# Four residual layers on one core: one more set of a recurrence's idle-time gate products, a full last block and ten fuller blocks ahead of it

## The chip, the cores and the metric

The kernel runs on one core of a Trainium2 chip. The metric is device microseconds of one execution; the profile is one execution taken by the hardware profiler. Where the text says PE it means TensorE, PEld its weight loads, DVE is VectorE, ACT ScalarE, POOL GpSimd, SP the queue that issues most DMAs.

## The reference

`x` is (16 batches, 512 steps, 512 features), `cond` is (16, 512), all float32. Four layers are added to x in turn:

```python
x = x + L0(x)    # wavelet analysis and synthesis with one gate per batch and feature: x + (x + x * gate)
x = x + L1(x)    # h = tanh(x_t @ Wx + b + h_prev @ Wh), 512 steps in sequence
x = x + L2(x)    # gates of all steps:
    f = sigmoid(x @ W_f.T + b_f); i = sigmoid(x @ W_i.T + b_i)
    s = f + i + EPS; f, i = f / s, i / s
    new = i * (x @ W_h.T + b_h)
    # log-cumulative sums of f and a scaled cumulative sum of new over the steps
x = x + L3(x)    # x + x @ (base + A_b @ B_b.T), a layer of rank 8 made per batch
```

L2's gates need only the finished x of the same step, so they can be computed while L1 is still working on later steps. That is what the change is about.

## The kernel before

**Two stages.** The first, lines 567 to 673, runs L0 and the recurrence L1: 64 blocks (`NBLK`) of 8 steps (`T`), all 16 batches at once. The second, the loop over batches behind `rnn.close()`, runs L2 and L3 batch by batch. Features stand in four chunks (`KC`) of 128 partitions. The result of the first stage, `x2`, stays on the chip as [128, 4, 16, 512].

**A step of the recurrence.** PE adds sixteen products of the previous h with `wh_sb` (L417, each of 32 columns, four beside each other) into a PSUM bank that already holds the input products; ACT takes tanh in four pieces (L609), DVE transposes each (L610), and the next step's products can begin. Behind its own products a step issues filler: input products of the next block (`inputs`, by the table `SHARE`; from block 17 on, four of sixteen in each odd step and none in the even ones), and parts of gates (`early_gate`).

**Parts and sets.** A set in `SETS` is (four batches, 128 steps, one chunk of 128 features) in all but the first few. It takes twelve parts: for f, i and the candidate four each, one for each chunk of the contraction. A part is four products of 512 columns (L465; float32, so each is two instructions on PE), with 32 output partitions each, side by side. `PARTS` says which steps of a block take a part; the sets are worked off in the order of the list. From block 17 to 62 that is steps 0, 2, 4, 6, in the last block 0, 2, 3, 4, 6. Input products end with block 62, since there is no next block.

**What follows a part.** After the fourth part of f its sigmoid runs on ACT six steps later, after the fourth of i at once (both L479), through `timed`. DVE then has sixteen pieces for a set: two sums (L489), eight reciprocals of 64 columns (L492), two products with f and two with i (L496), and, as `urgent`, two candidate products (L500). `do_pieces` takes one piece in each step, two in the last two blocks, and what is left is done behind the loop, ahead of `add_base` (L539), which makes batch 0's layer. Finished f and i go to `early` in DRAM from SP (L483). The PSUM of f, i and candidate alternates between two banks.

**The second stage.** `gate_unit(b, j)` computes one chunk of one batch. `made_before` gives the number of steps `te` that the sets have covered; for those f and i are loaded from `early` (SP, L715), and PE computes only columns `te` to 512 (L700: 24 instructions a unit, of 512 - te columns). ACT takes the sigmoids (L716), DVE sums, inverts, multiplies (L717 to L722) and runs three scans over all 512 columns (L726, L730, L732), POOL adds (L736, L737) into `x3`. Batches 0 to 7 have te = 128, 128, 144, 160 in their four chunks, batches 8 to 15 have 192, 192, 144, 160. After the second unit of a batch, PE runs the last product of the batch before (`last_layer`, L756), whose four tiles ACT copies (L751, two buffers `osb`) and SP stores (L752). Engines work their instructions off in order, so ACT's sigmoids of the third unit stand behind the copies, and a store on SP stands behind the loads of f and i that were issued before it; those wait for a free buffer (three for f, two for i).

Of the kernel before, what the change touches and what calls it, by code (L numbers as in the profile page):

```python
# [37 lines left out]
KC = D // P  # L38
R = 8

T = 8
NBLK = S // T
# [14 lines left out]
FIRST, SECOND, MAIN = 16 // T, 32 // T, 128 // T + 1  # L57
SETS = [(slice(0, 16), slice(0, 16), KC - 2), (slice(0, 16), slice(0, 32), KC - 1)]
# [2 lines left out]
SETS += [(slice(b, b + 4), slice(0, 128), j) for b in (0, 4) for j in range(KC - 2)]  # L61
SETS += [(slice(b, b + 4), slice(16, 144), KC - 2) for b in (0, 4, 8, 12)]
SETS += [(slice(b, b + 4), slice(32, 160), KC - 1) for b in (0, 4, 8, 12)]
SETS += [(slice(b, b + 4), slice(64, 192), j) for b in (8, 12) for j in (0, 1)]

PARTS = [()] * FIRST + [(0, 1, 3, 4, 5, 7)] * (SECOND - FIRST) + [(0, 2, 4)] * (MAIN - SECOND) + [(0, 2, 4, 6)] * (NBLK - MAIN - 1) + [(0, 2, 3, 4, 6)]
TE = 192


def made_before(b, j):  # L70
# [13 lines left out]
def kernel(  # L84
# [27 lines left out]
    def col(which, j):  # L112
        return vec_sb[:, which * KC + j : which * KC + j + 1]
# [16 lines left out]
    dram = ctx.enter_context(tc.tile_pool(name="dram", bufs=1, space=bass.MemoryType.DRAM))  # L130
    early = dram.tile([B, 2, KC, P, TE], F32, name="early")
    bias_a = dram.tile([R, D], F32, name="bias_a")
# [236 lines left out]
    def layer_part(i, k):  # L369

        if k == 0:
            layer_part.ps = ps_p.tile([P, P], F32, tag="pf", name=f"pf_{i}")
            if i:
                which, r = LAYERS[i]
                layer_part.bias = w2pool.tile([P, P], F32, tag="b2", name=f"b2_{i}", bufs=2)
                row = (bias_a, b2b)[which][r].rearrange("(j o p) -> j o p", j=KC, o=1)
                nc.sync.dma_start(out=layer_part.bias, in_=row.to_broadcast([KC, BP, P]))
        columns, src = (straight, hT3) if i else (tile_columns, aeT)
        for j in range(KC):
            nc.tensor.matmul(  # L380
                layer_part.ps[j * BP : (j + 1) * BP, :],
                src[:, k, :],
                columns(chunk_sb[i * KC + k], j),
                start=(k == 0),
                stop=(k == KC - 1),
                skip_group_check=True,
            )
        load_chunk()
# [46 lines left out]
    timed, urgent, pieces = {}, [], []  # L435
# [9 lines left out]
    def early_gate(q, step):  # L445

        u, k = divmod(q, KC)
        number, which = divmod(u, 3)
        batches, steps, j = SETS[number]
        shape = dict(b=batches.stop - batches.start, t=steps.stop - steps.start)  # L450
        width = shape["b"] * shape["t"]
        first = number < NSETS
        if k == 0:

            pool, tag = ((ps_q, "pg"), (ps_p, "pf"))[0 if first else (u - 3 * NSETS) % 2]
            early_gate.ps = pool.tile([P, WIDE], F32, tag=tag, name=f"pg_{u}")[:, :width]
            if which == 0:
                early_gate.tiles = [
                    w2pool.tile([P, WIDE], F32, tag=name, name=f"{name}_{number}")[:, :width]
                    for name in ("ef", "ei", "es")  # L460
                ]
        ps = early_gate.ps
        w = (wf_sb, wi_sb, wc_sb)[which]
        for c in range(KC):
            nc.tensor.matmul(  # L465
                ps[c * BP : (c + 1) * BP, :].rearrange("p (b t) -> p b t", **shape),
                w[:, k, j * P + c * BP : j * P + (c + 1) * BP],
                x2[:, k, batches, steps],
                start=(k == 0),
                stop=(k == KC - 1),  # L470
                skip_group_check=True,
            )
        if k < KC - 1:
            return
        f, i, s = early_gate.tiles
        halves = [slice(at, at + WIDE // 2) for at in range(0, width, WIDE // 2)]

        def sigmoid(gate, bias):
            nc.scalar.activation(gate, ps, AF.Sigmoid, bias=col(bias, j))  # L479

        def store(which, got, at):
            n = slice(at.start // shape["t"], at.stop // shape["t"])
            nc.sync.dma_start(  # L483
                out=early[batches, which, j, :, steps].rearrange("b p t -> p b t")[:, n],
                in_=got.rearrange("p (b t) -> p b t", **shape)[:, n],
            )

        def total(at):
            nc.vector.scalar_tensor_tensor(s[:, at], f[:, at], EPS, i[:, at], ALU.add, ALU.add)  # L489

        def invert(at):
            nc.vector.reciprocal(s[:, at], s[:, at])  # L492

        def normalize(which, at):
            got = (f, i)[which]
            nc.vector.tensor_tensor(got[:, at], got[:, at], s[:, at], ALU.mult)  # L496
            store(which, got, at)

        def times_candidate(at):
            nc.vector.scalar_tensor_tensor(  # L500
                i[:, at], ps[:, at], col(C_BH, j), i[:, at], ALU.add, ALU.mult
            )
            if at is halves[-1]:
                pieces.extend(lambda at=at: normalize(1, at) for at in halves)

        def end_input_gate():
            sigmoid(i, C_BI)
            early_gate.sums = [lambda at=at: total(at) for at in halves]
            pieces.extend(early_gate.sums)
            for n in range(0, width, WIDE // 8):  # L510
                pieces.append(lambda at=slice(n, n + WIDE // 8): invert(at))
            pieces.extend(lambda at=at: normalize(0, at) for at in halves)

        if which == 0:

            timed.setdefault(step if first else step + 6, []).append(lambda: sigmoid(f, C_BF))
        elif which == 1:
            timed.setdefault(step, []).append(end_input_gate)
        else:

            assert not any(job in pieces for job in early_gate.sums)
            urgent.extend(lambda at=at: times_candidate(at) for at in halves)
# [42 lines left out]
    for n in range(NBLK):  # L565
# [3 lines left out]
        for s in range(T):  # L569
# [16 lines left out]
            if s in LAYER_STEPS[n]:  # L586
                layer_part(n, LAYER_STEPS[n].index(s))
            if s in PARTS[n]:
                early_gate(made, n * T + s)
                made += 1  # L590
# [27 lines left out]
            if s == max(PAIRS[g]):  # L618
                t0, t1 = PAIRS[g]
                step = t1 - t0  # L620
# [250 lines left out]
```

## Time and profile before

| | us |
|---|---|
| three runs | 1618.48, 1618.99, 1623.41 (median 1618.99) |
| the profiled execution | 1615.84 |
| its span, first to last instruction | 1614.1 |
| PE, PEld, DVE, ACT, POOL busy | 1603.6, 1146.0, 1132.3, 424.9, 172.6 |
| recurrence | to 909 us of the span |
| loop over batches | from 909 us on |
| granted TensorE clock | 1.000 |

The profile's page gives the busy time of each engine, the chain that ended last and the costliest groups. A group's line holds the source line, engine, operation, tiles and shape, then busy time, mean duration and idle time of the engine ahead of it with what ended it. The timeline lists instructions by start and length; runs of the same instruction are merged, and a number in brackets is idle time before it and its releaser.

### The profile page before, as it was taken

How to read it: one execution, taken by the hardware profiler on the slowest of the kernel's cores; microseconds unless marked ns; L12 is line 12 of the kernel's file. 1: busy time of each engine (PE TensorE's matmuls, PEld its weight loads, DVE VectorE, ACT ScalarE, POOL GpSimd, SP SyncE). 2: the span in 40 equal slices, each digit the busy share in tenths (PEclk: the TensorE clock that was granted, in tenths of full speed). 3: DMA queues.
4: the chain of work that ended last, by engine and by line, in shares of the span. 5: the costliest groups of instructions: out<-in, count | busy, mean ns of one | idle time of the engine just before them, and what ended most of it. 6: DMA issues, size and time to landing. Idle time of an engine off the chain costs nothing.

```text
span 1614.1 us, 67901 instructions
## 1 busy us (share of the span) xinstructions
PE 1603.6 (99%) x29328; PEld 1146.0 (71%) x29328; DVE 1132.3 (70%) x3618; ACT 424.9 (26%) x2484; POOL 172.6 (11%) x145
## 2 busy tenths in 40 slices
PE   9999999999999999999999999999999999999998
PEld 6888888888888888888888655555555555555564
DVE  4555655565556666666665798888888888988887
ACT  3333333333333333333333211111111111111111
POOL 0000000000000000000000022222222222222222
PEclk9999999999999999999999999999999999999999
DMA  7554431111111111111111101111111111111111
GB/s 228 148 147 128 121 105 46 36 31 36 37 37 37 37 37 37 37 37 31 37 39 30 29 21 43 33 43 39 43 40 44 44 46 39 31 44 47 37 44 58
DMA packets 128085, 88.11 MB, mean 55 GB/s; under 512 B 22645, under 2 KB 116633, under 8 KB 127785
## 3 DMA queue, kind: packets, MB, share of 16 engines
q1 hardware_dynamic: 79152, 55.05, 11.1%
q10 hardware_dynamic: 48632, 28.73, 6.2%
q8 instruction: 229, 3.75, 1.0%
q14 instruction: 72, 0.58, 0.1%
HBM read 55.67 MB, written 28.07 MB: 52 GB/s over the span
## 4 chain that ended last, share of the span: by engine, by line
PE 96%; DVE 2%; DMA 1%; issue 0%; SPq 0%; ACT 0%; ACTq 0%; DVEq 0%
PE pre L417 41%; PE po L756 13%; PE pg L465 13%; PE pf L700 9%; PE pc L700 9%; PE pi L700 9%; PE pf L380 1%; PE pl_layer L535 1%; DVE s L718 1%; DMA wh_sb<-in_wh_dram 1%; PE pl_last L756 0%; DMA xb<-in_xT_dram 0%; DVE s L726 0%; DVE s L730 0%; PE po_last L756 0%
## 5 line engine op out<-in xcount | busy, mean ns | idle before, releaser
L417 PEld LDWEIGHTS pre<-wh_sb,h_out 128*32 128x32 f32 x16384 | 466.7, 110 | 146.6 <-DVE h_out L610 143.4
L417 PE MATMUL pre<-wh_sb,h_out 128*32 128x128 f32 x16384 | 560.6, 273 | 2.4 <-DVE h_out L610 1.1
L610 DVE STREAM_TRANSPOSE h_out<-a 128x32 f32<-128x32 f32 x2048 | 264.6, 187 | 347.4 <-ACT a L609 345.9
L609 ACT ACTIVATE a<-pre 128x32 f32<-128x32 f32 x2048 | 238.0, 203 | 573.4 <-PE pre L417 572.7
L417 PE MATMUL pre<-wx_sb,x 128*32 128x128 f32 x8192 | 285.9, 273 | 1.0 <-DMA wx_sb<-in_wx_dram 0.5
L417 PEld LDWEIGHTS pre<-wx_sb,x 128*32 128x32 f32 x8192 | 239.0, 110 | 2.1 <-DMA wx_sb<-in_wx_dram 1.5
L756 PE MATMUL po<-wx_sb,x 128*128 128x512 f32 x480 | 209.0, 592 | 0.1
L756 PEld LDWEIGHTS po<-wx_sb,x 128*128 128x128 f32 x480 | 91.0, 190 | 111.6 <-issue 105.7
L700 PE MATMUL pf<-x,wf_sb 128*128 128x352 f32 (+3 forms) x512 | 165.3, 466 | 0.3 <-DVE x L622 0.3
L700 PE MATMUL pc<-x,wc_sb 128*128 128x352 f32 (+3 forms) x512 | 163.7, 463 | 1.3 <-DVE i L722 1.3
L700 PE MATMUL pi<-x,wi_sb 128*128 128x352 f32 (+3 forms) x512 | 163.6, 462 | 0.0
L718 DVE RECIPROCAL s<-s 128x368 f32<-128x368 f32 (+2 forms) x64 | 152.2, 2378 | 2.2
L700 PEld LDWEIGHTS pf<-x,wf_sb 128*128 128x128 f32 x512 | 96.0, 190 | 68.4 <-issue 15.8
L736 POOL TENSOR_TENSOR s<-s,f 128x512 f32<-128x512 f32 x63 | 86.5, 1374 | 509.9 <-DVE s L730 504.1
L700 PEld LDWEIGHTS pc<-x,wc_sb 128*128 128x128 f32 x512 | 97.2, 190 | 57.5 <-DVE i L722 1.9
L700 PEld LDWEIGHTS pi<-x,wi_sb 128*128 128x128 f32 x512 | 97.3, 190 | 55.9
L622 DVE TENSOR_TENSOR x<-x,h_out 128x128 f32<-128x128 f32 x256 | 101.2, 395 | 18.9 <-DMA wi_sb<-in_wiT_dram 0.2
L751 ACT COPY osb<-po 128x512 f32<-128x512 f32 x60 | 35.1, 585 | 263.4 <-PE po L756 144.9
L683 POOL MEMSET zero<- 128x1 f32 x1 | 0.1, 98 | 907.5 <-DVE wx_sb L539 907.5
L717 DVE SCALAR_TENSOR_TENSOR s<-f,i 128x368 f32<-128x368 f32 (+2 forms) x64 | 34.7, 543 | 88.1 <-ACT i L716 88.1
L716 ACT ACTIVATE f<-pf,vec_sb 128x368 f32<-128x368 f32 (+2 forms) x64 | 35.7, 558 | 215.2 <-PE pf L700 160.6
L465 PE MATMUL pg<-x,wc_sb 128*32 128x512 f32 (+1 forms) x640 | 84.2, 581 | 0.0
(113 smaller groups left out, 1270.8 us busy)
## 6 DMA issues: line engine op xcount, KB each, us to landing
out_dram<-osb SPq DMA_DIRECT2D x63, 256.0 KB
xb<-in_xT_dram ACTq DMA_DIRECT2D x61, 256.0 KB
w<-in_l3w_dram SPq DMA_DIRECT2D x72, 128.0 KB
w<-in_l3w_dram ACTq DMA_DIRECT2D x64, 128.0 KB
early<-ef SPq DMA_DIRECT2D x39, 128.0 KB
early<-ei SPq DMA_DIRECT2D x39, 128.0 KB
f<-early SPq DMA_DIRECT2D x16, 96.0 KB
i<-early SPq DMA_DIRECT2D x16, 96.0 KB
```

Of the source, the lines that this page charges most:

```text
L417: nc.tensor.matmul(pre[PLACE[g][0]][j * BP : (j + 1) * BP, PLACE[g][1], :], lhsT, tile_columns(w, j), start=False, stop=False, skip_group_ ...
L465: nc.tensor.matmul(ps[c * BP : (c + 1) * BP, :].rearrange("p (b t) -> p b t", **shape), w[:, k, j * P + c * BP : j * P + (c + 1) * BP], x2 ...
L609: nc.scalar.activation(a[:, at], pre[bank][:, place, at], AF.Tanh)
L610: nc.vector.transpose(turned[:, c, :], a[:, at])
L622: nc.vector.tensor_tensor(x2[:, :, :, at].rearrange("p k b t -> p k t b"), xs[n][:, :, t0 // 2, :, :], turned.rearrange("p k (t b) -> p k ...
L700: nc.tensor.matmul(p[:, te:], w_sb[:, k, j * P : (j + 1) * P], x2[:, k, b, te:], start=(k == 0), stop=(k == KC - 1),)
L716: nc.scalar.activation(gate[:, new], p[:, new], AF.Sigmoid, bias=col(bias, j))
L717: nc.vector.scalar_tensor_tensor(s[:, new], f[:, new], EPS, i[:, new], ALU.add, ALU.add)
L718: nc.vector.reciprocal(s[:, new], s[:, new])
L736: engine.tensor_tensor(s, s, f, ALU.add)
L751: nc.scalar.copy(osb, po)
L756: nc.tensor.matmul(po, x3[:, k, t * P : (t + 1) * P], layer[:, k, :], start=(k == 0), stop=(k == KC - 1))
```

## The change

One set is added in the list: steps 128 to 255 of batches 4 to 7 in chunk 0, ahead of the last four sets. `made_before` follows the list, so these four units get te = 256 in place of 128. The twelve parts that it needs are placed by `PARTS`: the last block takes a part in each of steps 0 to 6, and each of the ten blocks ahead of it takes one more in step 7, behind that step's input products. The buffer `early` in DRAM grows to 256 steps a row (`TE`). The sigmoid of f now runs at the latest in the step before the first part that writes the same PSUM bank again (`FIRST_PARTS`).

```diff
 SETS += [(slice(b, b + 4), slice(32, 160), KC - 1) for b in (0, 4, 8, 12)]
+SETS += [(slice(4, 8), slice(128, 256), 0)]
 SETS += [(slice(b, b + 4), slice(64, 192), j) for b in (8, 12) for j in (0, 1)]
 
-PARTS = [()] * FIRST + [(0, 1, 3, 4, 5, 7)] * (SECOND - FIRST) + [(0, 2, 4)] * (MAIN - SECOND) + [(0, 2, 4, 6)] * (NBLK - MAIN - 1) + [(0, 2, 3, 4, 6)]
-TE = 192
+PARTS = [()] * FIRST + [(0, 1, 3, 4, 5, 7)] * (SECOND - FIRST) + [(0, 2, 4)] * (MAIN - SECOND)
+PARTS += [(0, 2, 4, 6)] * (NBLK - MAIN - 11) + [(0, 2, 4, 6, 7)] * 10 + [tuple(range(T - 1))]
+TE = 256
+
+SLOTS = [n * T + s for n in range(NBLK) for s in PARTS[n]]
+FIRST_PARTS = SLOTS[::KC]
+assert len(SLOTS) == 3 * KC * len(SETS)
...
-            timed.setdefault(step if first else step + 6, []).append(lambda: sigmoid(f, C_BF))
+            late = step if first else min(step + 6, FIRST_PARTS[u + 2] - 1)
+            timed.setdefault(late, []).append(lambda: sigmoid(f, C_BF))
```

The sets behind the new one start twelve parts later in the count of parts, but the added places make up for that: the last set now has its parts in blocks 62 and 63, where it had them in blocks 61 to 63.

## The prediction

> **What bounds the kernel now.** I read the page first, then the groups by shape, then the timeline of PE by step and of all engines at two places.
>
> ```profile
> span 1614.1 us, 67901 instructions
> ...
> PE 1603.6 (99%) x29328; PEld 1146.0 (71%) x29328; DVE 1132.3 (70%) x3618; ACT 424.9 (26%) x2484; POOL 172.6 (11%) x145
> ...
> PE pre L417 41%; PE po L756 13%; PE pg L465 13%; PE pf L700 9%; PE pc L700 9%; PE pi L700 9%; PE pf L380 1%; PE pl_layer L535 1%; DVE s L718 1%; DMA wh_sb<-in_wh_dram 1%; PE pl_last L756 0%; DMA xb<-in_xT_dram 0%; DVE s L726 0%; DVE s L730 0%; PE po_last L756 0%
> ```
>
> The chain that ended last is 96% PE, in the recurrence (L417, L465, to 909 us) and behind it (L700, L756). So what the change is worth is PE time added in the first stage less PE time removed in the second, unless another engine takes over.
>
> The recurrence, as PE's timeline shows it from step 7 of block 60 to step 1 of block 61 (start us, length, instruction):
>
> ```profile
> 865.47 1.09 PE L417 MATMUL pre<-wh_sb,h_out 128*32 128x128 f32 x32
> 866.34 1.09 PE L417 MATMUL pre<-wx_sb,x 128*32 128x128 f32 x32
> 867.21 1.09 PE L417 MATMUL pre<-wh_sb,h_out 128*32 128x128 f32 x32
> 868.09 1.07 PE L465 MATMUL pg<-x,wc_sb 128*32 128x512 f32 x8
> 868.94 1.09 PE L417 MATMUL pre<-wh_sb,h_out 128*32 128x128 f32 x32
> ```
>
> Starts, not lengths, count: ends are modelled and overlap. A step's own products take 0.87, the input products of odd steps 0.87, one part of even steps 0.86 (868.94 - 868.09). Each step has one filler behind its own products, while ACT and DVE make the next h. A filler costs little there because a step without any is hardly shorter. The last block shows that: it has no input products, and no part in its steps 1 and 5.
>
> ```profile
> 903.01 0.47 ACT L609 ACTIVATE a<-pre 128x32 f32<-128x32 f32 x4 [1.27 <-PE pre L417]
> ...
> 904.74 0.47 ACT L609 ACTIVATE a<-pre 128x32 f32<-128x32 f32 x4 [1.27 <-PE pre L417]
> ...
> 905.24 1.08 PE L417 MATMUL pre<-wh_sb,h_out 128*32 128x128 f32 x32 [0.56 <-DVE h_out L610]
> ...
> 906.39 0.47 ACT L609 ACTIVATE a<-pre 128x32 f32<-128x32 f32 x4 [1.18 <-PE pre L417]
> ```
>
> Step 4 (with a part) to 5: 904.74 - 903.01 = 1.73. Step 5 (empty) to 6: 1.65, with PE idle for 0.56. Over the block the starts give 1.645 and 1.643 for empty steps and 1.732 for steps with a part.
>
> Behind the recurrence, the groups by shape (busy us, mean ns):
>
> ```profile
> L465 PE MATMUL pg<-x,wc_sb 128*32 128x512 f32 x608 | 81.8, 592 | 0.0
> ...
> L700 PE MATMUL pf<-x,wf_sb 128*128 128x384 f32 x128 | 44.0, 487 | 0.3 <-DVE x L622 0.3
> ...
> L700 PE MATMUL pf<-x,wf_sb 128*128 128x320 f32 x128 | 37.2, 433 | 0.0
> ```
>
> PE's batch period there is 45.00 us for batches 1 to 7 and 42.44 for 8 to 11. Those differ by 128 columns over the four units of a batch (1488 against 1360), at 24 instructions a unit: 2.56 us, or 0.833 ns a column and instruction.
>
> **The change, part by part.**
>
> Two parts in the last block, steps 1 and 5: 2 x (1.732 - 1.644) = +0.18.
>
> Ten parts in step 7 of blocks 53 to 62. That step already holds input products, so PE has no idle left; the part comes whole: 10 x 0.858 = +8.58 (0.858 is 1.732 less the 0.873 of a step's own products).
>
> *A rule against it.* The Trainium skill, "TensorE: Matmul & The Clock Gate", section "Measured speedup vs the span model", gives 2.38 times for three 32-column tiles at once. Here four such tiles do a part's eight 512-column instructions in 0.86 us, and two full-width 512-column instructions of the last product take 13.73/32 x 2 = 0.86, so the trace shows the full four times. By the rule's share (2.38/3) a part would cost 1.08, an estimate, and the sum would be 2.7 us worse; the row decides.
>
> Sigmoids. In the built order three steps now hold both sigmoids of a set on ACT: 56.2 and 61.0 (with a bias copy as well) and 63.2. Before, they were two steps apart. An i sigmoid ended at 897.72 with the next tanh at 897.90, 0.18 later. One more f sigmoid (0.71) ahead of it fits only partly: tanh 0.47 + copy 0.31 + 0.71 + 0.69 = 2.18 against 1.73, with starts overlapping by some 0.13 each. Queued behind are the tanh, the transposes and PE. I bound each at 0 to 0.3 and take 0.1: +0.3.
>
> The new set's DVE pieces (16, about 7.6 us) and its four stores on SP go in steps where DVE is busy about 0.6 and SP idle: nothing, covered by the wait for tanh. If that cover went, 7.6. Pieces are emptied later at the end: three reciprocals (0.47 each) and one product (0.36) more stand between the last h and the four additions L539, 1.77 us. ACT's first sigmoid waited for those (at 912.74) and moves to 914.5; the input sigmoid, due at 914.84, moves by some 0.3, DVE's first unit by as much. PE needs that bank only at 917.22. Nothing on PE, and batches 1 to 3 have slack (below).
>
> Shorter units: batches 4 to 7, chunk 0, 384 to 256 columns: 4 x 24 x 128 x 0.833 ns = -10.24, the 45.00 to 42.44 step for four batches. 256 columns take 0.213 us an instruction, and a weight load 0.19 (L700 PEld), so loads still hide.
>
> **What is late next.** From batch 8 PE is no longer alone. Batch 13, third unit:
>
> ```profile
> 1495.50 1.20 DVE L730 TENSOR_TENSOR_SCAN s<-i,zero 128x512 f32<-128x512 f32 x1
> ...
> 1498.08 0.32 SPq L715 DMA_DIRECT2D f<-early  x1
> ...
> 1498.45 3.25 SPq L752 DMA_DIRECT2D out_dram<-osb  x3
> 1500.76 0.58 ACT L751 COPY osb<-po 128x512 f32<-128x512 f32 x1 [7.90 <-DMA out_dram<-osb]
> 1501.24 0.57 ACT L716 ACTIVATE f<-pf,vec_sb 128x368 f32<-128x368 f32 x1
> 1501.70 0.57 ACT L716 ACTIVATE i<-pi,vec_sb 128x368 f32<-128x368 f32 x1
> 1502.38 0.54 DVE L717 SCALAR_TENSOR_TENSOR s<-f,i 128x368 f32<-128x368 f32 x1 [5.68 <-ACT i L716]
> ```
>
> It is a loop: the output stores stand on SP behind a load of f that waits for POOL and so for DVE; ACT's copy waits for the stores (7.90); the sigmoids stand behind the copy; DVE idles 5.68 for them, and its next four units free the next f. The starts of L717 in the third units tell its period: 44.00 from batch 1 to 2 (wide units), 42.79, 42.81, 42.96, 42.92 for batches 8 to 11, mean 42.87, against PE's 42.44. So x3 gets later by 0.43 a batch: POOL ends a batch's fourth unit 12.8 to 13.2 us after PE's products at batches 3 to 7, then 13.14, 13.50, 14.03, 14.51, 15.48. There it stops, for PE's L756 waits for it (2.2 us in all), and PE's own period is 42.8 and 42.9 at batches 13 and 14.
>
> With the change, batches 4 to 7 have the DVE work of the later ones (the reciprocal is linear: 2553 ns at 384, 2153 at 320). The lag then grows from batch 4, its 2.6 us are used up four batches sooner, and PE pays 4 x 0.43 = +1.72.
>
> **The sum:** 0.18 + 8.58 + 0.3 - 10.24 + 1.72 = +0.54. The profiled execution took 1615.84 (span 1614.1 and 1.74 around it), which makes 1616.4; the median shown is 1618.99, 3.15 above it, and the same step from there is 1619.5. Moving a set from one stage to the other is nearly free of gain on PE (12 x 0.858 = 10.30 against 10.24); only the two empty steps win, 1.54, and the loop takes that back.
>
> **The rivals.**
>
> *The loop binds harder (slower).* If batches 4 to 7 keep the loop of 44.00 seen for wide units, PE saves 1.0 a batch, not 2.56: the sum is 9.06 - 4.0 = +5.1, 1624.1. For it: scans and other full-width work don't shrink. Against: batches 8 to 11 have the same column sum and show 42.87. It is slower by over 0.3% from a loop of 43.96 on. Chance 0.08.
>
> *The part of step 7 hides (faster).* If it cost 0.088, as in an empty step, the ten are 0.9 and the sum is -7.2: 1611.8. For it: even steps end on a wait for h. Against: odd steps show no such idle, PE is full there. Chance 0.04.
>
> *The lag never comes due, no sigmoid collides:* -1.5, 1617.5. It lies in the forecast's range. *The units are not shortened:* +9.1, 1628.1; against it, the built program has the 256-column products. Chance 0.01.
>
> **How the numbers follow.** About 0.3% (4.9 us) is what a measurement of this kernel can tell from no change. The forecast, with its bounds from -1.5 (above) to +2.4 (three collisions at 0.3, and two more disturbed loops like the 43.50 of batch 11 to 12, 0.63 each), is within it: 0.87. The runs shown spread over 4.9 us, so a median may stand 2.5 off either way: 1615.0 to 1624.1 as the range (1618.99 - 1.5 - 2.5; 1618.99 + 2.4 + 2.5, and on to the slower rival). From the cases: faster 0.05, same 0.86, slower 0.09.
>
> **What would show it.** In the profile after: steps 7 of blocks 53 to 62 at 2.60 where 1.747 stood; block 63 with no 1.645; its last h 9 us later; PE's batch period 42.44 from batch 4; POOL's lag growing from there and reaching 15.5 by batch 10; L717's period 42.9. A step 7 of 1.8, a batch period over 43.5 in batches 4 to 7, or a PE wait for i or f there would prove me wrong.

## The result and the profile after

| | before | after |
|---|---|---|
| median (runs) | 1618.99 (9, 1617.63 to 1623.41) | 1623.49 (9, 1620.32 to 1628.36) |
| profiled execution | 1615.84 | 1620.32 |
| its span | 1614.1 | 1618.5 |
| last tanh of the recurrence | 908.12 | 918.71 |
| from there to the end | 705.98 | 699.79 |
| granted clock of the profiled execution | 1.000 | 0.999 |

The ratio is 1.0027, with a 95% interval of 1.0017 to 1.0037: 4.4 us slower, 2.8 to 6.0. That is slower than the +0.54 forecast, within the range, and by the median within the 0.3% (4.9 us) that the forecast called no change; the interval reaches beyond it. The profiled execution is the shortest of those after, and the one before is shorter than any of the nine before; the two spans differ by 4.4 as well.

In the changed kernel the lines of the recurrence's products, parts and sigmoids stand 6 lower (L417 is L423, L465 is L471, L479 is L485), those behind them 7 lower (L609 is L616, L700 is L707, L716 is L723, L717 to L722 are L724 to L729, L736 and L737 are L743 and L744, L751 and L752 are L758 and L759, L756 is L763).

The page after: span, busy times, and the chain that ended last by engine and by line.

```profile
span 1618.5 us, 68138 instructions
...
PE 1609.2 (99%) x29424; PEld 1150.4 (71%) x29424; DVE 1134.1 (70%) x3634; ACT 424.7 (26%) x2486; POOL 172.1 (11%) x145
...
PE 94%; DVE 4%; DMA 1%; issue 1%; ACT 0%; SPq 0%; POOL 0%; ACTq 0%; DVEq 0%
PE pre L423 42%; PE pg L471 13%; PE po L763 12%; PE pf L707 8%; PE pc L707 8%; PE pi L707 8%; DVE s L725 1%; PE pf L386 1%; PE pl_layer L542 1%; DMA xb<-in_xT_dram 1%; DVE s L733 1%; DVE s L737 1%; PE pl_last L763 0%; DMA wx_sb<-in_wx_dram 0%; DVE i L736 0%
```

PE's share of the chain fell from 96% to 94%, and DVE's rose from 2% to 4%, in lines of the second stage (L725, L733, L737) above all: the chain passes through DVE more often.

**The recurrence did what the sum said.** PE's timeline in step 7 of block 62 shows the order that the prediction described, with the part (L471) in line behind the two groups of products, and nothing hidden.

```profile
902.86 1.06 PE L423 MATMUL pre<-wh_sb,h_out 128*32 128x128 f32 x32
903.73 1.06 PE L423 MATMUL pre<-wx_sb,x 128*32 128x128 f32 x32
904.61 1.04 PE L471 MATMUL pg<-x,wi_sb 128*32 128x512 f32 x8
905.47 1.06 PE L423 MATMUL pre<-wh_sb,h_out 128*32 128x128 f32 x32
```

905.47 - 902.86 = 2.61, where 1.747 stood. Blocks 53 to 62 take 147.72 instead of 139.13, block 63 takes 12.12 instead of 11.95: +8.59 and +0.17, together +8.76, the +0.18 and +8.58 of the sum to within 0.01 each.

The third term, a collision of sigmoids, did not come. ACT in the last block, where both sigmoids of the last set stand between two tanh:

```profile
910.05 0.46 ACT L616 ACTIVATE a<-pre 128x32 f32<-128x32 f32 x4 [1.27 <-PE pre L423]
910.38 0.71 ACT L485 ACTIVATE ef<-pg,vec_sb 128x512 f32<-128x512 f32 x1
910.95 0.72 ACT L485 ACTIVATE ei<-pg,vec_sb 128x512 f32<-128x512 f32 x1
911.78 0.47 ACT L616 ACTIVATE a<-pre 128x32 f32<-128x32 f32 x4
```

911.78 - 910.05 = 1.73, a step's usual length. From one instruction's start to the next's the f sigmoid takes 0.57, not 0.71, and the tanh 0.33, so all of it fits. The other two places cost nothing either.

The remaining +1.83 of the last tanh's +10.59 lies in blocks 0 to 16, which the change leaves alone: from the first tanh to the first of block 17 they took 238.8 before and 240.7 after, and anywhere from 238.8 to 244.8 in the profiles of this study. Two profiles alone can't resolve less than that; over all profiles the last tanh is at 908.1 to 913.5 with the old recurrence (six profiles, mean 911.6) and at 918.0 to 923.9 with the new one (eight, mean 920.5): +8.9.

**The second stage gave 6.2 instead of 8.5.** PE's batch period is 42.44 in batches 4 to 6, as said. Batch 7's is 42.94: PE is then ahead of the others and has to wait. Its waits for POOL ahead of the last product (us in total, times, longest; 1254 to 1552 us before, to 1560 after) are twice those of before, the first line before and the second after:

```profile
PEld po L756 <- POOL x L737: 2.2, 4, 0.9
...
PEld po L763 <- POOL x L744: 4.5, 6, 0.9
```

The starts of L724 in third units give the loop's periods:

| third unit, to batch | 4 | 5 | 6 | 7 | 8 | 9 | 10 | 11 | 12 | 13 | 14 |
|---|---|---|---|---|---|---|---|---|---|---|---|
| before | 45.00 | 45.00 | 45.37 | 44.63 | 42.79 | 42.81 | 42.96 | 42.92 | 43.50 | 42.87 | 42.95 |
| after | 43.29 | 43.17 | 43.28 | 43.22 | 42.86 | 42.94 | 42.85 | 42.91 | 44.26 | 42.90 | 42.86 |

The four legs to batches 4 to 7 sum to 172.96 against 180.00: -7.04. At the 42.87 of the prediction they would sum to 171.48, 1.48 less. The leg to batch 12 is 0.76 longer. -7.04 + 0.76 = -6.28, of the -6.2 measured. POOL ends a batch's fourth unit 12.7, 13.6, 14.3, 15.1, 15.5 us after PE's products at batches 3 to 7: the lag is used up at batch 7, not 10.

So two things were to be explained: why the loop with a 256-column unit takes 43.24 and not 42.87, and what makes the leg to batch 12 long. DVE and POOL in batch 4's first unit, from the timeline:

```profile
1095.16 0.40 DVE L724 SCALAR_TENSOR_TENSOR s<-f,i 128x256 f32<-128x256 f32 x1
...
1095.32 1.37 POOL L743 TENSOR_TENSOR s<-s,f 128x512 f32<-128x512 f32 x1 [7.33 <-DVE s L737]
...
1095.59 1.75 DVE L725 RECIPROCAL s<-s 128x256 f32<-128x256 f32 x1
...
1096.77 1.26 POOL L744 TENSOR_TENSOR x<-s,x 128x512 f32<-128x512 f32 x1
1097.38 0.93 DVE L726 TENSOR_TENSOR f<-f,s 128x256 f32<-128x256 f32 x1
```

And the groups by shape of batches 4 to 7 (busy us, mean ns):

```profile
L726 DVE TENSOR_TENSOR f<-f,s 128x256 f32<-128x256 f32 x4 | 3.7, 928 | 0.1
...
L726 DVE TENSOR_TENSOR f<-f,s 128x384 f32<-128x384 f32 x4 | 2.2, 557 | 0.1
```

The product f * 1/s takes 0.93 for 256 columns and 0.56 for 384. With 256 columns the reciprocal lasts only 1.75, and the product behind it starts at 1097.38, while POOL's addition of the unit before (1096.77 to 1098.03) still runs. It ends 0.28 after that. This is theory A: the shorter unit meets POOL's addition, and the product waits for it inside its own duration.

### The profile page after: what moved, and what is told of

Read it like the earlier page. It is cut to its first block, busy times and chain, and to the rows that moved or that the text cites. A ratio compares the mean times of both kernels' runs of the same rounds, so it can differ in the third digit from the quotient of the medians.

```text
span 1618.5 us, 68138 instructions
## 1 busy us (share of the span) xinstructions
PE 1609.2 (99%) x29424; PEld 1150.4 (71%) x29424; DVE 1134.1 (70%) x3634; ACT 424.7 (26%) x2486; POOL 172.1 (11%) x145
## 4 chain that ended last, share of the span: by engine, by line
PE 94%; DVE 4%; DMA 1%; issue 1%; ACT 0%; SPq 0%; POOL 0%; ACTq 0%; DVEq 0%
PE pre L423 42%; PE pg L471 13%; PE po L763 12%; PE pf L707 8%; PE pc L707 8%; PE pi L707 8%; DVE s L725 1%; PE pf L386 1%; PE pl_layer L542 1%; DMA xb<-in_xT_dram 1%; DVE s L733 1%; DVE s L737 1%; PE pl_last L763 0%; DMA wx_sb<-in_wx_dram 0%; DVE i L736 0%
## 5 line engine op out<-in xcount | busy, mean ns | idle before, releaser
L423 PEld LDWEIGHTS pre<-wh_sb,h_out 128*32 128x32 f32 x16384 | 465.9, 110 | 154.0 <-DVE h_out L617 145.7
L423 PE MATMUL pre<-wh_sb,h_out 128*32 128x128 f32 x16384 | 558.9, 273 | 1.8 <-issue 1.2
L616 ACT ACTIVATE a<-pre 128x32 f32<-128x32 f32 x2048 | 238.1, 203 | 582.3 <-PE pre L423 581.3
L423 PE MATMUL pre<-wx_sb,x 128*32 128x128 f32 x8192 | 285.0, 273 | 1.1 <-DMA wx_sb<-in_wx_dram 0.6
L423 PEld LDWEIGHTS pre<-wx_sb,x 128*32 128x32 f32 x8192 | 238.3, 110 | 2.2 <-DMA wx_sb<-in_wx_dram 1.4
L763 PE MATMUL po<-wx_sb,x 128*128 128x512 f32 x480 | 209.8, 593 | 0.1
L763 PEld LDWEIGHTS po<-wx_sb,x 128*128 128x128 f32 x480 | 90.8, 190 | 112.7 <-issue 103.6
L707 PE MATMUL pf<-x,wf_sb 128*128 128x352 f32 (+4 forms) x512 | 163.6, 463 | 0.0
L707 PE MATMUL pc<-x,wc_sb 128*128 128x352 f32 (+4 forms) x512 | 160.3, 456 | 0.5 <-DVE i L729 0.5
L707 PE MATMUL pi<-x,wi_sb 128*128 128x352 f32 (+4 forms) x512 | 160.2, 456 | 0.0
L725 DVE RECIPROCAL s<-s 128x368 f32<-128x368 f32 (+3 forms) x64 | 149.0, 2328 | 2.2
L707 PEld LDWEIGHTS pf<-x,wf_sb 128*128 128x128 f32 x512 | 96.7, 191 | 65.3 <-issue 14.5
L743 POOL TENSOR_TENSOR s<-s,f 128x512 f32<-128x512 f32 x63 | 86.0, 1365 | 502.4 <-DVE s L737 502.4
L707 PEld LDWEIGHTS pc<-x,wc_sb 128*128 128x128 f32 x512 | 97.2, 190 | 53.3 <-DVE i L729 1.0
L707 PEld LDWEIGHTS pi<-x,wi_sb 128*128 128x128 f32 x512 | 97.4, 190 | 52.7 <-issue 0.4
L758 ACT COPY osb<-po 128x512 f32<-128x512 f32 x60 | 35.1, 585 | 273.0 <-DMA out_dram<-osb 140.0
L724 DVE SCALAR_TENSOR_TENSOR s<-f,i 128x368 f32<-128x368 f32 (+3 forms) x64 | 34.1, 532 | 83.8 <-ACT i L723 83.8
L723 ACT ACTIVATE f<-pf,vec_sb 128x368 f32<-128x368 f32 (+3 forms) x64 | 35.3, 552 | 201.5 <-PE pf L707 143.8
L471 PE MATMUL pg<-x,wc_sb 128*32 128x512 f32 (+1 forms) x672 | 88.0, 582 | 0.0
```

The costliest lines, as they stand in the source:

```text
L423: nc.tensor.matmul(pre[PLACE[g][0]][j * BP : (j + 1) * BP, PLACE[g][1], :], lhsT, tile_columns(w, j), start=False, stop=False, skip_group_ ...
L471: nc.tensor.matmul(ps[c * BP : (c + 1) * BP, :].rearrange("p (b t) -> p b t", **shape), w[:, k, j * P + c * BP : j * P + (c + 1) * BP], x2 ...
L616: nc.scalar.activation(a[:, at], pre[bank][:, place, at], AF.Tanh)
L707: nc.tensor.matmul(p[:, te:], w_sb[:, k, j * P : (j + 1) * P], x2[:, k, b, te:], start=(k == 0), stop=(k == KC - 1),)
L723: nc.scalar.activation(gate[:, new], p[:, new], AF.Sigmoid, bias=col(bias, j))
L724: nc.vector.scalar_tensor_tensor(s[:, new], f[:, new], EPS, i[:, new], ALU.add, ALU.add)
```

## The experiments

Theory A prices the width. Its rivals: the loop is longer there because of where these batches stand, or because of the loads of f and i; and the denser steps of the recurrence cost clock or time elsewhere. The first four kernels tell these apart.

**The set is made but not used.** The changed kernel with the units left at their old widths:

```diff
-    return max(... if b in range(B)[batches] and chunk == j)
+    return max(... if b in range(B)[batches] and chunk == j and steps != slice(128, 256))
```

> The changed kernel with the new set made and stored as it is, but not used: batches 4 to 7 keep 128 columns made before, so every unit of the loop over batches is as wide as in the kernel before. Theory (the recurrence costs what its parts cost): the last h stands 8.75 us later (ten steps of 2.605, no step of 1.645), POOL's lag and the third-unit period in the loop are those of before (45.0 in batches 4 to 7), the total is 8 to 9.5 us over before. Rival (the loss lies in the recurrence, in pieces, stores or clock that follow from denser steps): more than 10 us over before, or a granted clock in the timed runs that is lower than that of before by 0.001 or more.

Measured: 1629.32 (1628.06 to 1630.35), ratio 1.0064 (1.0052 to 1.0076), +10.4 us, 8.4 to 12.3. That is over the 8 to 9.5 expected and, by the number, on the rival's side of 10; the interval takes in both, and the profile says where the surplus lies. In it blocks 53 to 62 take 147.72 and block 63 takes 12.12 as in the changed kernel, the legs to batches 4 to 7 are 45.0, POOL's lag is that of before, and the granted clock over the timed runs is 0.9988, as before. The recurrence's price is the 8.76 of the sum, and the denser steps by themselves take no clock, as far as five runs show. The surplus is in the second stage, 1.6 longer than before's; its leg to batch 12 is 45.08 where 43.50 stood.

**The units alone, once 256 and once twice 320 columns.** The kernel before, with batches 4 to 7 shortened by the same sum of columns, either in one unit or in two. The columns that no set has made are loaded from another tensor, so that part of the result is left out:

```diff
-        te = made_before(b, j)
+        made = made_before(b, j)
+        te = 256 if b in range(4, 8) and j == 0 else made      # units_256
+        te = 192 if b in range(4, 8) and j < 2 else made       # units_320
...
-            nc.sync.dma_start(out=gate[:, old], in_=early[b, which, j, :, old])
+            if te == made:
+                nc.sync.dma_start(out=gate[:, old], in_=early[b, which, j, :, old])
+            else:
+                nc.sync.dma_start(out=gate[:, old], in_=base[j * P : (j + 1) * P, old])
```

> The kernel before with its recurrence untouched; batches 4 to 7 compute only columns 256 to 511 in chunk 0, and the first 256 columns of f and i are loaded from the base layer's DRAM tensor instead of finished gates, so this part of the result is left out. Theory (the loop through the output stores sets the stage, and its period with a 256-wide and a 384-wide unit is 43.24): third-unit starts 43.2 to 43.3 apart in batches 4 to 7, product of f and 1/s 0.93 us in the 256-wide unit, total 6.3 to 7.5 us under before. As the prediction had it (42.87): 8.5 under before. If PE set the stage alone: 10.2 under before.

> The kernel before with its recurrence untouched; batches 4 to 7 compute columns 192 to 511 in chunks 0 and 1 (the same number of columns in all as with 256 and 384), and the columns ahead are loaded from the base layer's DRAM tensor, so this part of the result is left out. Theory (the 256-wide unit is too short for POOL's additions of the unit before, and its product waits for them): the third-unit period in batches 4 to 7 is 42.8 to 42.95 as in the later batches, no product over 0.62 us, total 8.0 to 9.0 us under before, 1.3 to 1.6 under the kernel with 256 and 384. Rival (the longer period belongs to batches 4 to 7 or to the larger load of f, not to the width of one unit): 43.2 here too, and the two kernels within 0.5 us.

| | time | ratio to before | legs to batches 4 to 7 | product f * 1/s |
|---|---|---|---|---|
| 256 | 1613.59 | 0.9965 (0.9954 to 0.9977) | 43.62 43.43 43.70 43.15 | 0.92 to 0.93 |
| 320, 320 | 1611.32 | 0.9957 (0.9944 to 0.9970) | 42.91 42.92 43.24 42.87 | 0.59 |

By the ratios the saving by itself is 5.7 us for the 256-column unit (3.7 to 7.4) and 7.0 for the two of 320 (4.9 to 9.1). Both are under what was expected (6.3 to 7.5 and 8.0 to 9.0), with intervals that take it in; both kernels have one more long leg, to batch 9 (43.92 and 44.11), of a kind that is taken up further down, with the leg to batch 12. With the two of 320 columns the same batches, with the same sum of columns computed and loaded, have legs of 42.99 on average, three of the four at 42.9. With the 256-column unit it is 43.48. So the width makes the period longer, not the place. The 256-column unit's legs here are 0.24 longer than the changed kernel's 43.24, though its product is as long; why is not shown. The two times by themselves, 1.3 apart with intervals that overlap, would not have settled it; the periods do. The wait accounts for most of the 0.37: the products of the first two units take 0.93 + 0.56 = 1.49 with 256 and 384 columns and 1.19 with 320 each, so 0.30 more. In the 320-column unit (timeline) the product starts only when POOL's addition is nearly done:

```profile
1141.83 2.15 DVE L722 RECIPROCAL s<-s 128x320 f32<-128x320 f32 x1
...
1143.00 1.27 POOL L741 TENSOR_TENSOR x<-s,x 128x512 f32<-128x512 f32 x1
...
1144.02 0.60 DVE L723 TENSOR_TENSOR f<-f,s 128x320 f32<-128x320 f32 x1
```

The reciprocal's 2.15 instead of 1.75 covers most of the addition, and 0.25 of it is left.

**The EPS split off ahead of the product.** In the 256-column units the constant is added to the loaded columns on their own, which was to move the product 0.3 later:

```diff
+        split = te == 256
+        if split:
+            nc.vector.tensor_scalar(f[:, old], f[:, old], EPS, None, ALU.add)
         nc.vector.tensor_tensor(f[:, new], f[:, new], s[:, new], ALU.mult)
-        nc.vector.tensor_scalar(f, f, EPS, None, ALU.add)
+        rest = f[:, new] if split else f
+        nc.vector.tensor_scalar(rest, rest, EPS, None, ALU.add)
```

> The changed kernel; in the four 256-wide units DVE adds EPS to the loaded columns of f between the reciprocal and the product with 1/s, and to the new columns behind it, so that POOL has 0.2 to 0.3 us more to end its addition into x3. Theory (the product takes 0.93 us because it waits for POOL): the product falls to 0.5 to 0.7 us, and the period in batches 4 to 7 from 43.24 to 43.0 to 43.2; the total moves by under 1 us against the changed kernel. Rival (a 256-wide product is slow by itself): 0.93 stays, and the period grows by 0.1 to 0.2 for one more instruction.

Measured: 1621.12, ratio 1.0015 (1.0005 to 1.0025); legs 43.10, 42.99, 43.07, 43.00. It decides nothing between the theories. The scheduler of the second stage moved the split addition ahead of the whole unit, so the product still starts right behind the reciprocal (1096.95, with the reciprocal at 1095.16) and still takes 0.93. The legs are some 0.2 shorter because the addition that is left on the path takes 0.28 and not 0.42.

The next four try both halves of the loop: the stores that bind ACT to DVE, and the product that waits.

**The output stores from ACT's queue.** Before, a store stands on SP behind the loads of f and i. From ACT's own queue it doesn't, and the loop is open. Done to both kernels, to see what the change would bring without the loop:

```diff
-        nc.sync.dma_start(out=out[b, t * P : (t + 1) * P, :], in_=osb)
+        nc.scalar.dma_start(out=out[b, t * P : (t + 1) * P, :], in_=osb)
```

> The kernel before with the output stores of all whole tiles issued from ACT's queue, right behind the copy that fills them, so that they no longer stand behind loads of f and i on SP. Theory (the loop over SP, ACT and DVE sets the second stage from batch 8 on): ACT's copies wait under 3 us for stores, third-unit starts 42.44 apart from batch 8 on as PE alone gives, POOL's lag stays at 13 us or less, total 2.5 to 4.5 us under before. Rival (DVE itself is full in these batches): the period stays at 42.8 and above and the total within 1 us.

> The changed kernel with the same edit to the output stores. Theory (the change wins 1.5 us of PE time and the loop takes it): third-unit starts 42.44 apart from batch 4 on, also with the product at 0.93 us, total 1 to 2.5 us under the kernel before with the same edit, so 4 to 6.5 under before. Rival (DVE's longer product sets the period of batches 4 to 7 without the loop, or the recurrence costs more than its parts): 43.2 stays, or the total is over the kernel before with the same edit.

The waits of the loop over batches (us in total, times, longest), in the changed kernel as it was:

```profile
ACT osb L758 <- DMA out_dram<-osb: 127.5, 20, 9.3
...
DVE s L724 <- ACT i L723: 64.3, 11, 7.1
```

and with the stores on ACT's queue:

```profile
ACT osb L758 <- PE po L763: 151.1, 44, 5.4
...
ACT i L723 <- PE pi L707: 77.5, 46, 1.9
```

The copy never waits for a store any more, only for PE, and the legs are 42.44 from batch 4 (from batch 8 in the kernel before), although the product still takes 0.93. So the loop through SP's queue is what turned DVE's 0.4 us into PE time. From the last tanh to the end the two kernels take 693.35 and 703.57: -10.22, all that PE's columns are worth. With the recurrence's +8.76 that would be -1.5 for the change without its loop. In time: 1615.77, ratio 0.9985 (0.9975 to 0.9996), or 2.4 us under before, for the kernel before with its stores moved, where 2.5 to 4.5 was expected, and 1617.11, 0.9982 (0.9972 to 0.9992), for the changed one, by the ratio 2.9 us under before (1.3 to 4.5) where 4 to 6.5 was expected. Between the two, -1.5 isn't resolved.

**The candidate ahead of the products.** The candidate's product reads one operand from PSUM. Placed directly behind the reciprocal, it runs while POOL's addition ends, and the product f * 1/s comes later:

```diff
-        nc.vector.tensor_tensor(f[:, new], f[:, new], s[:, new], ALU.mult)
-        nc.vector.tensor_scalar(f, f, EPS, None, ALU.add)
-        nc.vector.tensor_tensor(i[:, new], i[:, new], s[:, new], ALU.mult)
... (the candidate's product stands here)
+        nc.vector.tensor_tensor(f[:, new], f[:, new], s[:, new], ALU.mult)
+        nc.vector.tensor_scalar(f, f, EPS, None, ALU.add)
+        nc.vector.tensor_tensor(i[:, new], i[:, new], s[:, new], ALU.mult)
```

> The changed kernel with DVE's order in a unit altered: the candidate (one operand in PSUM) is added and multiplied right behind the reciprocal, ahead of the two products with 1/s. Theory (a product with both operands in SBUF waits while POOL adds): in the 256-wide units the product falls from 0.93 to 0.6 to 0.75 us and the period of batches 4 to 7 from 43.24 to 42.8 to 42.95; in the 320-wide ones from 0.59 to 0.53. Rival (the 256-wide product is slow by itself): 0.93 stays, and so does 43.24.

DVE and POOL in batch 4's first unit, as above:

```profile
1094.77 1.75 DVE L725 RECIPROCAL s<-s 128x256 f32<-128x256 f32 x1
...
1095.95 1.26 POOL L744 TENSOR_TENSOR x<-s,x 128x512 f32<-128x512 f32 x1
1096.44 0.39 DVE L726 SCALAR_TENSOR_TENSOR i<-pc,vec_sb,i 128x256 f32<-128x256 f32 x1
1096.75 0.75 DVE L729 TENSOR_TENSOR f<-f,s 128x256 f32<-128x256 f32 x1
```

The candidate's product goes through at 0.39 in the middle of POOL's addition. The product behind it still meets the end of it, 0.46 from 1096.75 to 1097.21, and ends 0.29 after it, as it ended 0.28 after it above. It takes 0.75 instead of 0.93. The legs to batches 4 to 7 are 42.79, 42.87, 42.80, 42.68 and some 42.3 behind them, but for 43.51 to batch 12; PE's batch period is 42.44 throughout; from the last tanh to the end it takes 693.28. The order saves time apart from the wait, too: by the groups by shape the candidate's own product takes 0.52 instead of 0.61 at 384 columns and 0.39 instead of 0.47 at 256. So the shorter legs are not the wait's alone. The time is 1615.64 (9 runs, 1613.12 to 1617.85), ratio to before 0.9986 (0.9976 to 0.9995): this one is a little faster than both kernels, 2.3 us below before (0.8 to 3.9) and 7.9 below the changed kernel by the medians, which were taken on different chips.

**POOL's additions moved away.** In one profiled execution, the additions of the fourth units of batches 3 to 6, which are the ones that the first units of batches 4 to 7 meet, run on DVE:

```diff
-        engine = nc.vector if (b, j) == (B - 1, KC - 1) else nc.gpsimd
+        engine = nc.vector if (b, j) == (B - 1, KC - 1) or (j == KC - 1 and 3 <= b < 7) else nc.gpsimd
```

> The changed kernel with both additions into x3 of the unit ahead of each 256-wide unit (fourth units of batches 3 to 6) on DVE in place of POOL, so POOL is idle while the 256-wide unit's product runs. Theory (the product waits for POOL): the product takes 0.42 to 0.5 us; the period of batches 4 to 7 grows by 0.7 to 1.0, since DVE has 1.38 us of additions more and 0.46 of waiting less. Rival (slow by itself): 0.93 stays and the period grows by 1.2 or more.

Groups by shape of batches 4 to 7:

```profile
L726 DVE TENSOR_TENSOR f<-f,s 128x256 f32<-128x256 f32 x4 | 1.6, 412 | 0.0
```

The same instruction, with the same operands, takes 0.41 when no addition runs on POOL beside it and 0.93 when one does. That shows theory A's wait, 0.52 a unit. The loop's legs were 43.68, 43.62, 43.71, 43.51, some 0.4 longer since DVE now does the additions, where 0.7 to 1.0 was expected; the time of the one run was 1625.7, and there is no interval to it.

**Repeated and combined.** The last four are the changed kernel again, and the two edits on each side.

> The changed kernel once more. Theory (8.75 us more in the recurrence, 7.04 less in the loop over batches, 0.8 lost where instruction fetches fall): 2 to 3 us over before. Rival (denser steps lower the granted clock as well, which showed as 0.9979 against 0.9989 in the runs so far): 4 to 6 over before again, with a mean clock again lower by 0.0007 or more.

> The kernel before with DVE's candidate ahead of the two products with 1/s. Theory (this order alone frees enough of DVE for PE to set the second stage): third-unit starts 42.3 to 42.45 apart from batch 8 on, total 1.5 to 3.5 us under before, and 0.5 to 2.5 over the changed kernel with the same order. Rival (the changed kernel gains from this order only because its own product waited): under 1 us from before.

> The kernel before with both edits, stores on ACT's queue and the candidate first. Theory: PE sets the stage already with one of them, so within 1 us of each alone, 2 to 4.5 under before.

> The changed kernel with both edits. Theory: within 1 us of the changed kernel with either one alone, and 1 to 2 us under the kernel before with both, which is the PE time that the two empty steps give. If the granted clock falls with denser steps, that difference is 0 or reversed.

`after_again` is the changed kernel as it is; `before_candidate_first` is the kernel before with the candidate moved as above; the last two have both edits, the candidate and the stores, in the kernel before and in the changed one.

| | time | ratio to before | last tanh to end |
|---|---|---|---|
| changed kernel again | 1624.10 | 1.0034 (1.0021 to 1.0046) | 699.52 |
| before, candidate first | 1617.55 | 0.9992 (0.9983 to 1.0001) | 703.34 |
| before, both | 1617.17 | 0.9991 (0.9981 to 1.0001) | 703.57 |
| changed, both | 1617.48 | 0.9989 (0.9981 to 0.9998) | 693.30 |

The changed kernel is again slower, by 5.5 us (3.4 to 7.4), with the second stage 6.5 shorter than before's: that is the rival's 4 to 6 with a lower clock, not the 2 to 3 of the theory. Moving the candidate in the kernel before shortens its second stage by 2.6 us, as much as moving the stores does, and the legs to batches 8 to 11 are 42.44, though its 384-column product takes the same as ever (0.56 and 0.55). Its candidate takes 0.45 instead of 0.54 at 320 columns, and the 320-column product 0.48 instead of 0.59. In time that is 1.3 us (-0.2 to 2.8), where 1.5 to 3.5 was expected. With both edits the stage is 10.3 shorter in the changed kernel, 8.76 given and 10.3 taken, but the times can't be told apart (0.3 us, in favour of the kernel before, where 1 to 2 the other way was expected).

**The granted clock, a rival for the rest.** 8.76 - 6.2 is 2.6, and the medians say 4.4 and 5.5. Both profiles of the changed kernel have a short stretch in which PE's clock was at half. The windows view (stretch, us, then PE, PEld, DVE, ACT and POOL busy with counts, PE's clock, DMA share, GB/s), of the changed kernel and of its repeat:

```profile
1464.00:1469.00 5.00, 5.00 (x12) 3.08 (x12) 4.97 (x7) 0.55 (x1) 0.00 (x0) 0.66 0.17 55
```

```profile
1467.00:1471.00 4.00, 4.00 (x9) 2.42 (x9) 3.97 (x5) 0.00 (x0) 0.00 (x0) 0.57 0.19 60
```

The half-clock stretch is 3.41 us long in both, at 1464.7 and 1467.6, right behind the same place: the third unit of batch 12, whose leg is the long one. The timeline there shows both that leg and why PE was less busy:

```profile
1458.25 0.32 SPq L722 DMA_DIRECT2D f<-early  x1
...
1458.62 4.66 SPq L759 DMA_DIRECT2D out_dram<-osb  x3
...
1462.33 0.58 ACT L758 COPY osb<-po 128x512 f32<-128x512 f32 x1 [9.32 <-DMA out_dram<-osb]
...
1462.97 1.12 PE L542 MATMUL po_layer<-bt,at 8*128 8x512 f32 x2 [0.41 <-ACT osb L758]
...
1463.96 0.54 DVE L724 SCALAR_TENSOR_TENSOR s<-f,i 128x368 f32<-128x368 f32 x1 [7.08 <-ACT i L723]
...
1464.02 4.33 PE L707 MATMUL pf<-x,wf_sb 128*128 128x352 f32 x8
```

It is the loop of the prediction again: ACT's copy waits 9.32 for the first of the three stores, DVE waits 7.08, PE waits 0.41 with only products of 8 rows about, and its next eight instructions take 4.33. With the set unused the same eight take 2.63.

What makes the leg long is the time from that store's issue to the copy that it holds up: 3.71 here (1462.33 - 1458.62) against 2.31 in batch 13 of before (1500.76 - 1498.45). The slow issue of the first store is not the cause in general: with the set unused, where the leg is 45.08, it is issued in 0.42, and the copy follows 4.51 after its issue began. The traces' packets show what goes with it. In the ten profiles with their stores on SP's queue, batches 8 to 13 make 60 such stores. Through 45 of them no instruction fetch runs, and the copy comes 2.23 to 2.44 behind the issue. Through five runs a fetch of 8 KB, and it comes after 2.63 to 2.93; through eight, fetches of 16 or 24 KB, 3.37 to 4.51. In the last two the fetch begins within 0.3 us of the copy, and nothing is late. Each leg is longer than its neighbours by as much as its store is late, to within 0.1. At batch 12 the kernels with the old recurrence have 8 KB there (legs of 43.20 to 43.50, and 42.72 with the candidate moved), those with the added set 16 or 24 KB (44.06 to 45.08, and 43.51 with the candidate moved). So the long legs go with the fetches, and the kernels with the added set have more of them at that place. That the fetches make the store late is not isolated: no run took them away.

The Trainium skill, "TensorE: Matmul & The Clock Gate", section "What's actually happening", says that the gate goes to half after an idle stretch of some 3.4 us. The length of the stretches here is that figure, but PE was not idle for any such time ahead of them, it was only doing little. With the set unused PE does as little at that place and waits 0.43, and its clock stays full.

What does the clock cost? Over the timed runs the mean granted clock is 0.9989 to 0.9992 for the kernel before, 0.9979 and 0.9974 for the changed kernel, 0.9981 with EPS split, 0.9988 with the set unused and 0.9990 with the candidate moved; with the stores on ACT's queue it is 0.9991 before and 0.9986 changed, with both edits 0.9991 and 0.9985. One stretch of 3.41 us at half clock is 0.001 of the span (3.41 / 2 / 1618.5). Eight of the fourteen profiles also have one of 3.41 or 6.83 us that begins 15 to 18 us into the span, five of them with the added set and three without. In 177 runs of the study, run by run against each kernel's mean, 0.001 of clock goes with 1.46 us (correlation -0.64). 0.0010 to 0.0018 less is then 1.5 to 2.6 us, about what is missing. That agrees, but it isn't isolated: no run changed the clock alone, and in the profile shown the stretch cost nothing. PE's batch 12 takes 45.95 by its own starts, but its next two take 42.44 where the loop's legs are 42.90 and 42.86: PE makes up for the stretch with what it would have waited.

## Why the prediction was right, and where its steps were off

The price of the recurrence and what PE gains were right, and so was the loop that takes most of the gain back. That the number holds is in part luck: +4.4 lies outside the forecast's own bounds of -1.5 to +2.4, and within the range only by the 2.5 allowed for the spread of medians. By the time alone it is nearer to the slower rival's +5.1 than to +0.54.

- **Two parts in the last block, +0.18; ten in step 7, +8.58:** right to 0.01 each, and shown alone by the set that is made and not used. The 0.858 a part came again, not the 1.08 of the rule that was weighed against it. The rival in which a part of step 7 hides is gone.
- **Three collisions of sigmoids, +0.3:** nothing was measured. The working added up durations less 0.13 an instruction; start to start, two sigmoids and a tanh take 1.73 at most and fit a step.
- **DVE's pieces and stores at nothing, the later end of the pieces at nothing:** right. Nothing in blocks 53 to 63 is longer than the parts explain.
- **PE's columns, -10.24:** right. PE's period is 42.44 until it has to wait in batch 7, and with the stores on ACT's queue or the candidate moved the whole of it reaches the end (693.3 against 703.3 to 703.6).
- **What is late next, +1.72:** the mechanism was right and the size was off; this is the step that failed. The loop of SP's stores, DVE and POOL takes the gain back, the lag grows from batch 4, and PE pays. But the period was taken as 42.87 "with the DVE work of the later ones (the reciprocal is linear)". The sum of DVE's durations was taken as a function of the columns, and one duration wasn't: the product takes 0.93 and not the 0.41 that it has alone, since a shorter reciprocal lets it begin while POOL's addition runs. The period is 43.24, the term 1.48 larger, and the lag is used up at batch 7, not 10. Nothing in the trace of before showed a 256-column unit, so this was an unknown cost, and it should have had a bound in the range.
- **The leg to batch 12:** allowed for in the upper bound ("two more disturbed loops, 0.63 each"), and it came once, +0.76, at a store that lands late beside instruction fetches. With 1.48 that makes -6.2 of the second stage where -8.5 was forecast.
- **The sum:** 8.76 - 6.2 = +2.6 instead of +0.54. Of the 4.4 by the medians (2.8 to 6.0) some 1.8 is left. In the two profiles it stands as 1.8 in blocks 0 to 16, which vary as much by themselves; there the clock was full in both, so in these two it isn't the clock. Over the timed runs the lower clock would account for it. What it is stays open.
- **The rivals:** the harder loop (44.00, +5.1) is the one that the period went towards: 43.24, 0.37 of the 1.13 that lay between the forecast's period and the rival's. Its reason, that full-width work doesn't shrink, isn't what did it.

The rule that explains the product is in the Trainium skill, "SBUF — State Buffer", section "SBUF: two separate sides": VectorE and GpSimd share a pair of ports as an exclusive lock, and a VectorE operation with two inputs in SBUF stands still until a GpSimd operation that reads SBUF is done. The runs agree: 0.93 with the addition beside it, 0.41 without, an end 0.28 to 0.35 behind the addition's end wherever it started, and 0.39 for the candidate's product, whose one operand is in PSUM.

## What to carry to other kernels

When a change makes one engine's instruction shorter, look at what its successor then starts beside, on POOL above all: the cost of the shorter unit isn't read from the longer one by columns alone. When an engine is freed, follow the loop that holds the next one (here a store queued on SP behind a load) and try to cut it there, or to put an instruction that doesn't collide into the gap; here one moved instruction made the changed kernel's second stage 6.5 us shorter, more than the set did. A sum of profiled rows was good to 0.01 where its rows were in the trace of before, and off where a shape was not.

## What was not expected of the hardware

- A wait of DVE for POOL doesn't show as idle time: it lies in the duration of the instruction, 0.93 against 0.41 us for the same product of 128 x 256. A group's mean that grows as its shape shrinks (0.56 at 384 columns, 0.93 at 256) gives it away.
- PE's clock fell to half for 3.41 us behind a stretch in which PE was only partly idle, at the same place in two executions; eight instructions took 4.33 us there, and 2.63 in an execution that did as little ahead of them and kept its clock.
- A store beside instruction fetches held the copy behind it for 2.63 to 4.51 us, where 2.23 to 2.44 is usual, in 13 of the 15 places where fetches ran. At batch 12 it did so in all ten profiles with their stores on SP's queue.
